# Products of weights with values of all four key tiles in one run behind the fourth exponential, and a new hand-searched order of the work

## The chip, the cores and the metric

The kernel runs on one core of a Trainium2 chip. The metric is the device time of one execution in microseconds (us). Before the change the median of three runs is 2063.27 us (2061.38 to 2065.82). A difference of about 0.2% or more can be told from no change.

The core has five engines, each of which takes its instructions in the order in which they stand in its own queue: TensorE (PE in the profile, its weight loads PEld), VectorE (DVE), ScalarE (ACT), GpSimd (POOL) and SyncE (SP, which here issues DMAs).

## The reference

Sixteen sequences of 512 positions with 256 features pass through one block, all in float32. Cut to what matters:

```python
x = x + attn(layernorm(x))      # 16 heads of 16 features, causal, softmax over the keys
x = x + ffn(layernorm(x))       # base product, shared and routed low-rank parts, 2 of 6 experts
x = x + ssm(layernorm(x))       # convolution, gates, scan over 512 positions with 16 states
x = x + ffn(layernorm(x))

# inside attn, for each head
scores = q @ k.T * scale        # masked above the diagonal
attn   = softmax(scores)
out    = attn @ v
```

The change concerns the inside of `attn`. The rest of the block matters because its operations stand in the same queues.

## The kernel before, in words

**Tiling.** A sequence is four tiles of 128 positions. The 16 heads are worked on in four groups of four heads (index `j`, `G = 4` heads). Keys and queries stand transposed in `kT` and `qT`, with the 16 features of a head in a strip of 32 partitions of its own, so four heads can use four row strips of TensorE's array at the same time.

**Scores.** The helper `four` (line 560) makes one batch of scores: four matmuls of 32 rows, one for each head (line 566, row strips), and four bfloat16 matmuls with the identity that add the causal mask (line 568, the whole array). All go to one PSUM tile named `sc`. This tile takes four of the eight PSUM banks and there is **one** of it: `banks = {"one": (4, ...), "sc": (1, ...)}`. The next batch can only start when the reader of the last one has finished. Each batch is made twice. In the first pass (mask_q, queries on the partitions, lines 628 to 640) VectorE reduces the batch to its maximum `negm` (line 637). The maxima go through a transpose (line 645) into the queries `qm` (line 650). In the second pass (mask_k, keys on the partitions, line 587 ff.) ScalarE takes the exponential of the batch and writes it to `pt0` to `pt3`, one SBUF buffer for each key tile (line 585). By causality the batches of the four key tiles have 512, 384, 256 and 128 columns a head. A sequence has 16 batches of the first kind and 16 of the second.

**Products with values.** Behind each exponential stands an operation `weigh` (line 588): four matmuls, one for each head, whose outputs go to four column strips of 32 partitions of one PSUM tile `one` (line 590, named `av`). Key tile 0 starts the sum, key tile 3 ends it. ScalarE then copies the sums to `avs` (line 596), TensorE transposes them (line 601) and VectorE divides (lines 608 and 609).

The array is thus used in three ways: in row strips (line 566), in column strips (line 590, the sums of the scan at line 874, and a small product at line 474 with 32 rows out), and whole (everything else on TensorE).

**Scan.** For each sequence, 32 groups of rows are fetched from DRAM (line 849), GpSimd multiplies (lines 856 and 867), ScalarE takes exponentials (line 861), VectorE runs the scan (line 864) and TensorE adds up (line 874).

**Order of the work.** Nothing runs in the order in which it is written. `Plan.op` records every operation with its engine, an estimated cost in microseconds (helpers `dve`, `act`, `pool`, `pe` at lines 459 to 470 and numbers beside the calls), what it reads and writes, and which buffers it takes. `Plan.order` (line 126) then walks through a model of the five engines: whenever one is free, it gives it the ready operation with the lowest turn whose buffers are free. The turn of an operation is `STARTS[sequence] + TURNS[number in the sequence]`; both tables stand in the file and were found by a search. Around a score batch an engine can be reserved: `o.then` names who is to go next, and another operation may delay that by at most `OVER` us (`kept`). `CHANGE` is a penalty in turns on an operation that needs another table of ScalarE. The instructions are issued in the order that this walk gives, and each engine keeps it.

Of the kernel before, what the change touches and what calls it, by code (L numbers as in the profile page):

```python
# [17 lines left out]
P = 128  # L18
NEG = -1.0e30


OVER, CHANGE = 2.3, 97.0
STARTS = (
    0, 149, 234, 338, 413, 521, 619, 700, 790, 888, 996, 1074, 1174, 1263, 1369, 1447,
)
TURNS = (
# [20 lines left out]
)  # L47
# [16 lines left out]
class Op:  # L64
    __slots__ = ("eng", "cost", "lat", "fn", "bufs", "after", "left", "seq", "turn", "num", "table", "load", "port", "then", "stage")


class Plan:
# [14 lines left out]

    def op(self, eng, cost, fn, r=(), w=(), lat=None, table=None, load=0.0, also=(), port=False):


        o = Op()
        o.eng, o.cost, o.fn, o.seq, o.num, o.table, o.load = eng, cost, fn, self.seq, len(self.ops), table, load
        o.lat = {"PE": 0.08, "ACT": 0.05, "SP": 2.0}.get(eng, 0.12) if lat is None else lat
        o.after, o.left, o.bufs = [], 0, []  # L90
        before = {}
        for things, writes in ((r, False), (w, True)):
            for thing in things:
                buf, part = thing if isinstance(thing, tuple) else (thing, None)
                if buf not in o.bufs:
                    o.bufs.append(buf)
                    buf.users += 1
                for p, (ws, rs) in buf.done.items():
                    if part is None or p is None or p == part:
                        for x in ws + (rs if writes else []):  # L100
                            before[x.num] = x
                ws, rs = buf.done.setdefault(part, ([], []))
                if not writes:
                    rs.append(o)
                elif part is None:
                    buf.done = {None: ([o], [])}
                else:
                    buf.done[part] = ([o], [])
        for buf in also:
            if buf not in o.bufs:  # L110
                o.bufs.append(buf)
                buf.users += 1
        before.pop(o.num, None)
        o.port, o.then, o.stage = port, None, self.stage
        for x in before.values():
            x.after.append(o)
            o.left += 1
        self.ops.append(o)
        return o
# [6 lines left out]
    def order(self):  # L126

        first = {}
        for o in self.ops:
            o.turn = STARTS[o.seq] + (TURNS or [0] * len(self.ops))[o.num - first.setdefault(o.seq, o.num)]  # L130
        free, busy, table, link, port = dict(self.places), {}, None, 0.0, False
        kept = {}
# [8 lines left out]
        while True:  # L141
            for eng, heap in ready.items():
# [28 lines left out]
                if o.table is not None:  # L171
                    cost += 1.3 * (o.table != table)
                    table = o.table
                if until is not None and self.wanted(o, what):
                    del kept[eng]
# [48 lines left out]
def tile_block(ctx: ExitStack, tc: tile.TileContext, a: dict, out: bass.AP):  # L224
# [231 lines left out]
    def rows(g):  # L456
        return slice(32 * g, 32 * g + 32)
# [4 lines left out]
    def act(n):  # L462
        return 0.2 + n / 1200.0

# [3 lines left out]
    def pe(n, k=1, extra=0.02):  # L468

        return k * 2 * (n / 1200.0 + extra)  # L470
# [28 lines left out]
    def turned(xh, xt, c, at, also=()):  # L499

        one = psum("one")

        def turn():
            for t in range(NT):
                nc.tensor.transpose(one()[:, cols(t)], xh()[:, t, cols(c)], ident)  # L505

        op("PE", 0.66, turn, r=[xh], w=[one], also=[xt, *also])
        op("ACT", act(512), lambda: nc.scalar.copy(xt()[:, c, at : at + T], one()), r=[one], w=[(xt, c)])
        return one
# [28 lines left out]
    def attention(b, x):  # L538
# [9 lines left out]
        for t in range(0, NT, 2):  # L548
# [5 lines left out]

            op("PE", pe(256, 4) + 0.2, value, r=[xt], w=[one], also=[vals])
            op("ACT", act(512), lambda t=t, one=one: nc.scalar.copy(
# [3 lines left out]
        def four(lhsT, rhs, at, mask, n, reads, into):  # L560
# [8 lines left out]

            o = op("PE", pe(n, 1, 0.09) + 0.45, run, r=reads, w=[sc], also=[into])  # L570
            return sc, o
# [3 lines left out]
        def weights_values(j, kT, qm):  # L575

            av, avs = psum("one"), sbuf("avs")
            for kt in range(NT):
                n = T - kt * P
                pt = sbuf(f"pt{kt}")  # L580
                sc, o = four(
# [5 lines left out]

                def weigh(kt=kt, pt=pt, av=av, j=j):
                    for g in range(G):
                        nc.tensor.matmul(  # L590
                            av()[rows(g), kt * P : T], lhsT=vals()[:, kt, G * j + g, :], rhs=pt()[:, g, :],
                            start=kt == 0, stop=kt == NT - 1,
                        )

                op("PE", pe(n, 1, 0.1), weigh, r=[pt, vals], w=[av], also=[avs])
            op("ACT", act(512), lambda avs=avs, av=av: nc.scalar.copy(avs(), av()), r=[av], w=[avs])
# [5 lines left out]

            op("PE", 0.66, back, r=[avs], w=[at], also=[o_tok])

# [8 lines left out]

            op("DVE", 0.72, divide, r=[at], w=[(o_tok, j)])

        for i in range(NJ // 2):
# [30 lines left out]
            qms = [sbuf("qm"), sbuf("qm")]  # L647
            op("PE", 0.66, turn, r=[nm], w=[one], also=qms)
            for s, qm in enumerate(qms):
# [7 lines left out]
        for c in range(NC):  # L657
# [5 lines left out]

            op("PE", 0.66, turn, r=[(o_tok, j) for j in range(NJ) if j * NC // NJ == c], w=[one], also=[oT])
            op("ACT", act(512), lambda c=c, one=one: nc.scalar.copy(oT()[:, c, :], one()), r=[one], w=[(oT, c)])
# [8 lines left out]
    def routed(x):  # L674
# [39 lines left out]

        op("DVE", 0.65, logits, r=[m1], w=[one])
        op("ACT", 0.25, lambda: nc.scalar.activation(ex(), lg(), AF.Exp), r=[one], w=[ex], table="exp")
# [5 lines left out]

        op("DVE", 0.65, first, r=[b1], w=[one, o1])

# [8 lines left out]

        op("DVE", 1.5, second, r=[ex, o1, m2, b2], w=[one])

# [7 lines left out]

        op("DVE", 1.3, shares, r=[ex, z, rz], w=[one, w7])
        op("DVE", 0.65, lambda: nc.vector.tensor_tensor(
# [10 lines left out]
        hT = sbuf("hT")  # L756
        op("PE", 0.66, turn, r=[hs], w=[pt], also=[hT])
        op("ACT", act(512), lambda: nc.scalar.copy(hT(), pt()[0 : NU + 1, :]), r=[pt], w=[hT])
# [7 lines left out]
    def scan(b, x):  # L766
# [71 lines left out]
        for c in range(NC):  # L838
            sums = psum("one")
            for m in range(4):  # L840
# [36 lines left out]

                op("PE", pe(512, 1, 0.18), add, r=[four[0], four[2]], w=[sums])

# [70 lines left out]
```

## Time and profile before

| | |
|---|---|
| median of 3 runs | 2063.27 us (2061.38 to 2065.82) |
| the profiled execution's own time | 2066.51 us |
| its span, first to last instruction | 2064.7 us |
| busy PE / PEld / DVE / ACT / POOL | 1801.9 / 953.8 / 1513.4 / 1194.0 / 1371.1 us |
| mean granted TensorE clock | 0.954 |
| DMA | 316.35 MB, mean 153 GB/s |

The profile gives times in us from the span's start. `L566` is line 566 of the kernel. A row such as `PE L566 MATMUL sc<-qm,kT 32*128 32x384 f32 x8` reads: matmuls of line 566 that write the tile `sc` from `qm` and `kT`, 32 rows and 128 columns of the array, a moving operand of 384 columns in float32, eight of them. A float32 matmul leaves two records, so eight records are the four matmuls of one batch. Matmuls overlap, and their ends are modelled; what one operation costs TensorE is therefore read here from the **start** of its first matmul to the start of the next operation's first. Some matmul records are missing from the trace.

### The profile page before, as it was taken

What the parts mean: (1) busy time and instruction counts of PE and PEld (TensorE: products, weight loads), DVE (VectorE), ACT (ScalarE), POOL (GpSimd) and SP (SyncE); (2) the same over time, 40 slices, a digit from 0 to 9 for tenths busy, and PEclk for the clock granted to TensorE, in tenths of its full rate; (3) what the DMA queues carried; (4) which work ended last, traced back from release to release, by engine and by line L of the source; (5) the groups of instructions that cost most, each with busy time, mean ns of one, the idle gap of its engine ahead of it and who ended that gap; (6) DMA issues with size and microseconds to landing.
All of it is one profiled execution on the core that took longest, in us unless ns stands there. A gap on an engine that the chain in (4) does not pass through costs nothing. (4 is left out here: it accounts for less than half of the span.)

```text
span 2064.7 us, 34733 instructions
## 1 busy us (share of the span) xinstructions
PE 1801.9 (87%) x13253; PEld 953.8 (46%) x13253; DVE 1513.4 (73%) x2479; ACT 1194.0 (58%) x1685; POOL 1371.1 (66%) x814
## 2 busy tenths in 40 slices
PE   4788789999999999999999999999999999996455
PEld 2244344555455454545455454545554454544123
DVE  4335677878788787878788787878788787876563
ACT  2236556565666757565666667575666766564431
POOL 3001784949587685859597785859596785848693
PEclk8789899999999999999999999999999999998766
DMA  3000956848494866847494867849493957747791
GB/s 93 1 1 22 216 122 155 197 127 210 109 233 109 216 164 167 205 137 191 110 231 100 225 153 175 204 120 212 110 231 95 228 143 186 183 125 183 186 222 31
DMA packets 113064, 316.35 MB, mean 153 GB/s; under 512 B 17809, under 2 KB 36610, under 8 KB 112898
## 3 DMA queue, kind: packets, MB, share of 16 engines
q1 hardware_dynamic: 112194, 313.99, 62.5%
q8 instruction: 105, 1.72, 0.4%
q14 instruction: 61, 0.50, 0.1%
q10 hardware_dynamic: 704, 0.14, 0.0%
HBM read 287.87 MB, written 26.21 MB: 152 GB/s over the span
## 5 line engine op out<-in xcount | busy, mean ns | idle before, releaser
L864 DVE TENSOR_TENSOR_SCAN dd<-one,dd 128x512 f32<-128x512 f32 x512 | 607.9, 1212 | 185.2 <-ACT one L861 88.3
L856 POOL TENSOR_TENSOR dd<-dd,bc 128x1024 f32<-128x1024 f32 x256 | 603.6, 2361 | 194.0 <-DMA dd<-drows 156.8
L867 POOL TENSOR_TENSOR dd<-dd,bc 128x1024 f32<-128x1024 f32 x256 | 601.9, 2358 | 86.2 <-DVE dd L864 80.4
L637 DVE TENSOR_REDUCE negm<-sc 128x4 f32<-128x512 f32 (+3 forms) x256 | 380.4, 1486 | 154.0 <-PE sc L568 153.7
L861 ACT ACTIVATE one<-dd,am 128x512 f32<-128x512 f32 x512 | 344.3, 689 | 249.4 <-DVE dd L864 108.9
L585 ACT ACTIVATE pt<-sc 128x2048 f32<-128x2048 f32 (+3 forms) x256 | 316.3, 1235 | 189.0 <-PE sc L568 187.8
L487 POOL TENSOR_SCALAR rs<-mv 128x4 f32<-128x4 f32 x64 | 12.3, 193 | 364.2 <-DVE mv L482 361.4
L566 PE MATMUL sc<-qm,kT 32*128 32x512 f32 (+3 forms) x2048 | 214.1, 488 | 37.8 <-ACT pt L585 28.4
L566 PE MATMUL sc<-kT,qT 32*128 32x128 f32 (+3 forms) x2048 | 217.0, 494 | 30.5 <-DVE negm L637 25.9
L568 PEld LDWEIGHTS <-identb 128*128 128x128 bf16 x2048 | 117.4, 98 | 232.4 <-issue 217.2
L874 PE MATMUL one<-dd,ysel 128*32 128x512 f32 x1024 | 172.7, 633 | 55.5 <-POOL dd L867 46.4
L590 PE MATMUL one<-pt,vv 128*32 128x512 f32 (+3 forms) x2048 | 191.6, 449 | 8.1 <-DVE dd L864 7.9
L566 PEld LDWEIGHTS sc<-qm,kT 32*128 32x128 f32 x2048 | 80.9, 185 | 181.5 <-ACT pt L585 120.4
L474 PE MATMUL one<-base,xtR 128*128 128x256 f32 x512 | 139.5, 395 | 18.6 <-DVE dd L864 18.0
L566 PEld LDWEIGHTS sc<-kT,qT 32*128 32x128 f32 x2048 | 82.0, 187 | 156.8 <-DVE negm L637 63.3
L494 ACT ACTIVATE xhR<-x,nm,rs 128x256 f32<-128x256 f32 x192 | 99.4, 588 | 53.2 <-POOL nm L490 53.1
L528 DVE TENSOR_TENSOR x<-one,x 128x512 f32<-128x512 f32 x128 | 86.4, 675 | 34.7 <-PE one L474 34.5
L474 PEld LDWEIGHTS one<-base,xtR 128*128 128x128 f32 x512 | 94.5, 194 | 36.8 <-DVE dd L864 21.5
L481 DVE BATCH_NORM_STATS2 st<-x 128x6 f32<-128x256 f32 x256 | 103.7, 405 | 4.8 <-DMA x<-in_x_dram 4.1
L568 PE MATMUL sc<-mask_q,identb 128*128 128x128 bf16 x1024 | 103.7, 225 | 0.0
L568 PE MATMUL sc<-mask_k,identb 128*128 128x128 bf16 x1024 | 102.8, 224 | 0.0
L505 PE MATMUL one<-ident,xhR 128*128 128x128 f32 x384 | 61.9, 290 | 35.2 <-ACT xhR L494 27.7
(132 smaller groups left out, 2449.4 us busy)
## 6 DMA issues: line engine op xcount, KB each, us to landing
dd<-drows SPq DMA_DIRECT2D x512, 512.0 KB
x<-in_x_dram SPq DMA_DIRECT2D x16, 512.0 KB
drows<-dt SPq DMA_DIRECT2D x32, 256.0 KB
drows<-sg SPq DMA_DIRECT2D x32, 256.0 KB
bc<-brows SPq DMA_DIRECT2D x16, 512.0 KB
out_dram<-x SPq DMA_DIRECT2D x16, 512.0 KB
brows<-few SPq DMA_DIRECT2D x16, 64.0 KB
wo<-in_Wo_dram SPq DMA_DIRECT2D x2, 256.0 KB
```

The costliest lines, as they stand in the source:

```text
L474: nc.tensor.matmul(o[:, lo:hi], lhsT=lhsT, rhs=rhs, start=n == 0, stop=n == len(todo) - 1)
L481: nc.vector.bn_stats(st()[:, t, :], x()[:, t, :])
L566: nc.tensor.matmul(sc()[:, g, 0:n], lhsT=lhsT(g), rhs=rhs(g), start=True, stop=False)
L568: nc.tensor.matmul(sc()[:, g, at : at + P], lhsT=identb, rhs=mask, start=False, stop=True)
L585: o.then = op("ACT", act(G * n), lambda pt=pt, sc=sc, n=n: nc.scalar.activation(pt(), sc()[:, :, 0:n], AF.Exp), r=[sc], w=[pt], table="exp")
L590: nc.tensor.matmul(av()[rows(g), kt * P : T], lhsT=vals()[:, kt, G * j + g, :], rhs=pt()[:, g, :], start=kt == 0, stop=kt == NT - 1,)
L637: o.then = op("DVE", dve(G * n), lambda t=t, n=n, sc=sc, nm=nm, s=s: nc.vector.tensor_reduce(nm()[:, t, :, 1 - s, 0:1], sc()[:, :, 0:n], A ...
L856: op("POOL", pool(1024), lambda dd=dd: nc.gpsimd.tensor_tensor(dd()[:, :, 1, :], dd()[:, :, 1, :], both(0), ALU.mult), port=True, r=[(bc, ...
L861: op("ACT", act(512) + 0.07, lambda i=i, k=k, dd=dd, dec=dec: nc.scalar.activation(dec(), dd()[:, i, 0, :], AF.Exp, scale=am[:, k + 4 * i ...
L864: op("DVE", 1.22, lambda i=i, dd=dd, dec=dec: nc.vector.tensor_tensor_scan(dd()[:, i, 1, :], dec(), dd()[:, i, 1, :], 0.0, ALU.mult, ALU.a ...
L867: op("POOL", pool(1024), lambda dd=dd: nc.gpsimd.tensor_tensor(dd()[:, :, 1, :], dd()[:, :, 1, :], both(1), ALU.mult), port=True, r=[(bc, ...
L874: nc.tensor.matmul(sums()[rows(g), :], lhsT=ysel[:, m, :], rhs=four[g]()[:, g % 2, 1, :], start=m == 0, stop=m == 3)
```

## The change

Each exponential had its product `weigh` behind it. Now the four products of a group of heads are one operation of 16 matmuls that reads all four of `pt0` to `pt3`. The matmuls, their shapes and their number are the same. The planner's costs are new numbers for many operations, its model of TensorE takes 0.2 us off an operation of "columns" mode behind another one, `OVER` goes from 2.3 to 1.7, `CHANGE` from 97 to 60, and both tables of turns are new. The core of the diff:

```diff
-OVER, CHANGE = 2.3, 97.0
+OVER, CHANGE = 1.7, 60.0
 STARTS = (
...
+                if eng == "PE":
+                    cost -= 0.2 * (o.mode is not None and o.mode == mode)
+                    mode = o.mode
...
     def act(n):
-        return 0.2 + n / 1200.0
+        return 0.17 + n / 1200.0
...
-        op("PE", 0.66, turn, r=[xh], w=[one], also=[xt, *also])
+        op("PE", 0.57, turn, r=[xh], w=[one], also=[xt, *also])
...
-            o = op("PE", pe(n, 1, 0.09) + 0.45, run, r=reads, w=[sc], also=[into])
+            o = op("PE", pe(n, 1, 0.0) + 0.5, run, r=reads, w=[sc], also=[into])
...
             av, avs = psum("one"), sbuf("avs")
+            pts = [sbuf(f"pt{kt}") for kt in range(NT)]
             for kt in range(NT):
                 n = T - kt * P
-                pt = sbuf(f"pt{kt}")
+                pt = pts[kt]
...
-                def weigh(kt=kt, pt=pt, av=av, j=j):
+            def weigh():
+                for kt in range(NT):
                     for g in range(G):
                         nc.tensor.matmul(
-                            av()[rows(g), kt * P : T], lhsT=vals()[:, kt, G * j + g, :], rhs=pt()[:, g, :],
+                            av()[rows(g), kt * P : T], lhsT=vals()[:, kt, G * j + g, :], rhs=pts[kt]()[:, g, :],
                             start=kt == 0, stop=kt == NT - 1,
                         )

-                op("PE", pe(n, 1, 0.1), weigh, r=[pt, vals], w=[av], also=[avs])
+            op("PE", 2.2 + 0.2, weigh, r=pts + [vals], w=[av], also=[avs], mode="columns")
...
-                op("PE", pe(512, 1, 0.18), add, r=[four[0], four[2]], w=[sums])
+                op("PE", pe(512, 1, 0.18), add, r=[four[0], four[2]], w=[sums], mode="columns")
```

The remaining edits are costs of the planner alone (a few hundredths to 0.2 us each, as in the third and fourth hunk), and the tables `STARTS` and `TURNS`. They change no instruction, only the order.

More of the change, by code (lines that the diff above doesn't have):

```diff
@@ L19 @@
 NEG = -1.0e30
-OVER, CHANGE = 2.3, 97.0
+OVER, CHANGE = 1.7, 60.0
 STARTS = (
-    0, 149, 234, 338, 413, 521, 619, 700, 790, 888, 996, 1074, 1174, 1263, 1369, 1447,
+    0, 363, 754, 1360, 1140, 1792, 2114, 2484, 3089, 2828, 3285, 3687, 3986, 4332, 4709, 4877,
 )
 TURNS = (
[20 rows of a table removed]
[22 rows of a table added]
 )
@@ L64 @@
 class Op:
-    __slots__ = ("eng", "cost", "lat", "fn", "bufs", "after", "left", "seq", "turn", "num", "table", "load", "port", "then", "stage")
+    __slots__ = ("eng", "cost", "lat", "fn", "bufs", "after", "left", "seq", "turn", "num", "table", "load", "port", "then", "stage", "mode")
 class Plan:
@@ L82, in buf, with op @@
         return Buf(self, res, make)
-    def op(self, eng, cost, fn, r=(), w=(), lat=None, table=None, load=0.0, also=(), port=False):
+    def op(self, eng, cost, fn, r=(), w=(), lat=None, table=None, load=0.0, also=(), port=False, mode=None):
         o = Op()
@@ L113, in op @@
         before.pop(o.num, None)
-        o.port, o.then, o.stage = port, None, self.stage
+        o.port, o.then, o.stage, o.mode = port, None, self.stage, mode
         for x in before.values():
@@ L130, in order @@
             o.turn = STARTS[o.seq] + (TURNS or [0] * len(self.ops))[o.num - first.setdefault(o.seq, o.num)]
-        free, busy, table, link, port = dict(self.places), {}, None, 0.0, False
+        free, busy, table, link, port, mode = dict(self.places), {}, None, 0.0, False, None
         kept = {}
@@ L553, in value @@
                     products(one()[:, i * D : (i + 1) * D], [(xt()[:, c, cols(t + i)], wv[:, c, :], 0, D) for c in range(NC)])
-            op("PE", pe(256, 4) + 0.2, value, r=[xt], w=[one], also=[vals])
+            op("PE", pe(256, 4), value, r=[xt], w=[one], also=[vals])
             op("ACT", act(512), lambda t=t, one=one: nc.scalar.copy(
@@ L601, in back @@
                     nc.tensor.transpose(at()[:, cols(t)], avs()[:, cols(t)], ident)
-            op("PE", 0.66, back, r=[avs], w=[at], also=[o_tok])
+            op("PE", 0.57, back, r=[avs], w=[at], also=[o_tok])
             def divide(at=at, j=j):
@@ L612, in divide @@
                 )
-            op("DVE", 0.72, divide, r=[at], w=[(o_tok, j)])
+            op("DVE", 0.68, divide, r=[at], w=[(o_tok, j)])
         for i in range(NJ // 2):
@@ L647, in attention @@
             qms = [sbuf("qm"), sbuf("qm")]
-            op("PE", 0.66, turn, r=[nm], w=[one], also=qms)
+            op("PE", 0.57, turn, r=[nm], w=[one], also=qms)
             for s, qm in enumerate(qms):
@@ L662, in turn @@
                     nc.tensor.transpose(one()[:, cols(t)], o_tok()[:, t, cols(c)], ident)
-            op("PE", 0.66, turn, r=[(o_tok, j) for j in range(NJ) if j * NC // NJ == c], w=[one], also=[oT])
+            op("PE", 0.57, turn, r=[(o_tok, j) for j in range(NJ) if j * NC // NJ == c], w=[one], also=[oT])
             op("ACT", act(512), lambda c=c, one=one: nc.scalar.copy(oT()[:, c, :], one()), r=[one], w=[(oT, c)])
@@ L713, in logits @@
             nc.vector.tensor_tensor(lg(), lg(), wide(m1()), ALU.subtract)
-        op("DVE", 0.65, logits, r=[m1], w=[one])
+        op("DVE", 0.57, logits, r=[m1], w=[one])
         op("ACT", 0.25, lambda: nc.scalar.activation(ex(), lg(), AF.Exp), r=[one], w=[ex], table="exp")
@@ L721, in first @@
             nc.vector.tensor_tensor(o1(), k1(), wide(b1()), ALU.is_equal)
-        op("DVE", 0.65, first, r=[b1], w=[one, o1])
+        op("DVE", 0.55, first, r=[b1], w=[one, o1])
         def second():
@@ L732, in second @@
             nc.vector.tensor_tensor(lg(), lg(), o1(), ALU.add)
-        op("DVE", 1.5, second, r=[ex, o1, m2, b2], w=[one])
+        op("DVE", 1.33, second, r=[ex, o1, m2, b2], w=[one])
         def shares():
@@ L742, in shares @@
             nc.vector.tensor_tensor(w7()[:, :, 0:E], lg(), wide(rz()), ALU.mult)
-        op("DVE", 1.3, shares, r=[ex, z, rz], w=[one, w7])
+        op("DVE", 1.1, shares, r=[ex, z, rz], w=[one, w7])
         op("DVE", 0.65, lambda: nc.vector.tensor_tensor(
@@ L756, in routed @@
         hT = sbuf("hT")
-        op("PE", 0.66, turn, r=[hs], w=[pt], also=[hT])
+        op("PE", 0.57, turn, r=[hs], w=[pt], also=[hT])
         op("ACT", act(512), lambda: nc.scalar.copy(hT(), pt()[0 : NU + 1, :]), r=[pt], w=[hT])
```

42 rows, old and new, of the table TURNS are left out of this document.

## Prediction

> **What bounds the kernel now.** I read the page's slices first, then the busy time by stretch, then the waits of TensorE in the even middle, then TensorE's order of time.
>
> ```profile
> PE   4788789999999999999999999999999999996455
> ...
> PEclk8789899999999999999999999999999999998766
> ```
>
> ```profile
> 600.00:1755.00 1155.00, 1087.82 (x8284) 581.11 (x8280) 936.18 (x1521) 740.95 (x1051) 853.70 (x500) 1.00 0.70 170
> 0.00:300.00 300.00, 225.63 (x1634) 113.41 (x1635) 148.07 (x261) 126.65 (x169) 95.02 (x77) 0.87 0.31 75
> 1843.00:2065.00 222.00, 123.76 (x576) 66.20 (x576) 121.78 (x207) 83.49 (x123) 157.04 (x81) 0.74 0.68 162
> ```
>
> The columns are PE, PEld, DVE, ACT, POOL, then clock and DMA. TensorE bounds the middle: 1087.8 of 1155 us busy at full clock, DVE 936, POOL 854, ACT 741. Ten sequences pass there: the first of a sequence's exponentials of scores comes every 115.5 us (mean of ten). Head and tail are looser. The chain of waits, taken from the end, covers the tail alone, so I work with TensorE's queue. Its longest wait in the middle is
>
> ```profile
> PE sc L566 <- ACT pt L585: 14.2, 50, 0.4
> ```
>
> that is, a score batch waiting for the exponential of the batch before it. Here is what stands around such waits:
>
> ```profile
> 1731.96 0.93 PE L566 MATMUL sc<-qm,kT 32*128 32x384 f32 x8 [0.20 <-ACT pt L585]
> 1732.82 0.40 PE L568 MATMUL sc<-mask_k,identb 128*128 128x128 bf16 x4
> 1733.80 1.06 PE L590 MATMUL one<-pt,vv 128*32 128x512 f32 x8 [0.58 <-DVE dd L864]
> 1734.80 0.71 PE L566 MATMUL sc<-qm,kT 32*128 32x256 f32 x8
> 1735.45 0.40 PE L568 MATMUL sc<-mask_k,identb 128*128 128x128 bf16 x4
> 1735.77 0.85 PE L590 MATMUL one<-pt,vv 128*32 128x384 f32 x8
> 1736.96 0.50 PE L566 MATMUL sc<-qm,kT 32*128 32x128 f32 x8 [0.33 <-ACT pt L585]
> ```
>
> From the 256-column batch (1734.80) to the next (1736.96) are 2.16 us. TensorE's own batch takes 0.97 of them; a product with values fills most of the rest. That product is **filler** while the one `sc` tile is being read.
>
> **What the change saves: switches.** Costs are taken start to start:
>
> ```profile
> 1000.68 0.40 PE L568 MATMUL sc<-mask_k,identb 128*128 128x128 bf16 x4
> 1001.01 0.85 PE L590 MATMUL one<-pt,vv 128*32 128x384 f32 x8
> 1001.68 1.04 PE L874 MATMUL one<-dd,ysel 128*32 128x512 f32 x8
> ...
> 1005.21 0.40 PE L568 MATMUL sc<-mask_q,identb 128*128 128x128 bf16 x4
> 1005.45 1.29 PE L505 MATMUL one<-ident,xhR 128*128 128x128 f32 x8
> ```
>
> A mask run takes 0.33 before column strips and 0.24 before the whole array; medians over the trace are 327 and 234 ns, so entering a strip mode costs 93 ns. The 384-column product takes 669 ns before other column-strip work (0.67 above) and 783 before whole-array work, 114 ns for leaving. The 256-column one has 456 and 570, the same 114. A run of column strips thus costs 207 ns beyond its work.
>
> The built order of both kernels (counted, no time in it) has the same 8,227 matmuls. Runs of column strips fall from 346 to 189; entries into row strips straight from whole-array work rise from 310 to 382. Sum: 157 x 0.207 = 32.5 saved, 72 x 0.093 = 6.7 given back, **25.8 us less TensorE work**. In the even middle, a sequence has 22 runs before and 12 after, 19 entries and 23: 2.07 - 0.37 = 1.70 us less. A run of four products (512, 384, 256, 128 columns) should take 0.88 (996 ns alone, less 114) + 0.67 + 0.46 + 0.36 = 2.37 us; four lone ones take 1.00 + 0.78 + 0.57 + 0.36 = 2.71. The joint behind 512 columns is too rare in the trace to show; between no gain and the 114 ns I take the latter, by the two joints it does show.
>
> [...]
>
> ScalarE loads its tables 16 times less (68 to 52, 1.283 us each, 20.5 us). ScalarE is idle a third of the middle, so I count it as nothing; if a load stood ahead of an exponential that a score batch waits for, it would be at most those 20.5. The products issue no DMA. All queues are reordered, SP's and GpSimd's among them, but the counts are equal, and before the first scan (133 against 138 us of TensorE work) and behind the last score batch (136 against 138 us of GpSimd work) they stand alike.
>
> **What it costs: the filler is gone.** A score batch can't start before the reader of the last one has finished. The shortest start-to-start times with that bound, from the trace, are for exponentials (512, 384, 256, 128 columns) 3.44, 2.80, 2.16, 1.52 us, and for maxima 3.86, 3.11, 2.36, 1.62. The batch itself, with both switches, is 1.40, 1.19, 0.97, 0.76 of each. The rest must be filled by whatever the order has between, or TensorE stands. I went through both orders, added the durations of everything between two batches, and took the shortfall.
>
> Even middle, one sequence, before: two batches of 512 (0.29, 0.32), one of 384 (0.61), two of 256 (0.40 each), two of 128 (0.19 each): 2.39 us. After: twice a batch of 384 and then one of 256 follow with **nothing** between: 2 x (2.80 - 1.19 + 2.16 - 0.97) = 5.58; a 512-maximum with only transposes (0.71); 0.32, 0.31, 0.20 and 0.17 elsewhere: 7.29 us. So a sequence costs 4.90 more in waits and 1.70 less in switches: **+3.19 us**.
>
> As a check, the same sum for before is 111.25 of work + 2.39 = 113.64 us; the trace has 115.5. The 1.9 us left are waits for other data, such as line 474 for VectorE. After: 116.83, or 118.7 with the same 1.9.
>
> The whole, to the last-but-one scan's start: before 1684.8 + 70.8 = 1755.6, after 1655.6 + 152.7 = 1808.3 us. Of the difference of **52.7**, 15.8 come from the head (up to the third scan 42.1 against 64.8 us of shortfall, 6.9 less work), 35.2 from eleven even sequences, 1.7 from the one after. Behind that point 160 us of GpSimd work stand in both orders, and I count zero.
>
> The profiled execution took 2066.5 (span 2064.7 and 1.8 around it), 3.2 above the median. 2066.5 + 52.7 - 3.2 = **2116 us**.
>
> The new wait for all four exponentials stands at the products. Behind it is all of TensorE's queue, the next score batch first. In 46 of 64 runs a later score batch stands between the fourth exponential and the products. In the other 18, about one a sequence, it is mostly a 512-column batch whose exponential ends 3.4 us from the batch's start, and 3.55 us of work stand there (1.31 + 1.72 + 0.44 + 0.09). So I price it at nothing; bounds are no gain and, if such an exponential starts its own length late, 18 x 1.87 = 34 us. The wait for other data (1.9 a sequence) is not shown for the new order: it can vanish under the longer score waits (-22 over twelve sequences) or double (+22).
>
> [...]
>
> **Rivals.**
> 1. *The waits swallow each other.* Waits for `sc` give other data time, the 1.9 vanish, and the head loses only half its 15.8: 2116 - 22 - 8 = 2086. For it: those waits name VectorE, idle 219 of 1155 us, which could catch up while TensorE stands. Against: VectorE has waits of its own for score batches, which come later too.
> 2. *The end pays* (other side: faster). In 1843 to 2065 GpSimd is busy 157 of 222 us, so 65 could go; the last slices show TensorE at 4 to 6 tenths. It decides from 53 us on; if all 65 went, 2116 - 65 = 2051. Against: the order there has the same GpSimd work, and GpSimd's waits there are for fetched rows first (22.6 us), which the change leaves alone.
> 3. *Score turnarounds don't bind, switches do*: 2063.3 - 25.8 = 2037. It needs a 384-column exponential to hand back `sc` in under 1.2 us, where it lasts 1.45 itself. That the change doesn't cut switches is excluded by the count.
> 4. *New waits*, on VectorE or behind the fourth exponential: 2116 + 22 to 34, near 2145.
>
> **Numbers.** Forecast 0.67 (2100 to 2132), rival 1 0.13, rival 4 0.08, near no change 0.03, rival 2 0.06, rival 3 0.03. A measurement here tells about 0.2% from no change. Faster 0.09, same 0.03, slower 0.88. The range 2083 to 2145 takes in rivals 1 and 4 and leaves out about 0.14.
>
> **What would show it.** Right: about 190 runs of column strips, 0.88/0.67/0.46 inside a run; score batches of 384 and 256 columns 2.8 and 2.2 us before the next with TensorE idle; its waits for `pt` well above 14 us in a like stretch; a period near 118.7 us; the tail unchanged. Wrong: a period under 115.5, or a tail (last-but-one scan to end, 221 us) shorter by tens.

## The result, and the profile after

After the change: 2153.23 us (2152.66 to 2156.31, four runs) against 2064.55 for before (2061.38 to 2065.90, four runs), a ratio of 1.0435 (1.0417 to 1.0453). The forecast was 2116 with a range up to 2145: slower, as said, but by 88.7 us instead of 52.7, and outside the range. From one scan to the next a sequence takes 120.7 us (mean of eleven; 115.4 before); the forecast was 118.7.

First the two rows of the page's slices for after.

```profile
PE   5688888898989899998889899898988899987634
...
PEclk8689998999999999999999999999999999997766
```

Before had a 9 in every slice of the middle's PE row; now 8s stand among them. The clock's digits look alike, since they stop at 9. The busy time by stretch (same columns as before: PE, PEld, DVE, ACT, POOL, clock, DMA) shows what they hide.

```profile
600.00:1755.00 1155.00, 1046.98 (x7927) 591.42 (x7926) 890.08 (x1448) 697.00 (x995) 830.84 (x479) 0.95 0.69 165
0.00:300.00 300.00, 219.63 (x1552) 114.03 (x1553) 136.43 (x233) 117.49 (x157) 84.07 (x72) 0.84 0.29 70
1927.00:2151.00 224.00, 131.18 (x600) 72.34 (x596) 120.51 (x210) 81.18 (x122) 157.12 (x81) 0.71 0.66 158
```

In the even middle the granted clock is 0.95 where it was 1.00, and TensorE is busy 1047 us of 1155 where it was 1088. Its longest wait, in the same stretch:

```profile
PE sc L572 <- ACT pt L592: 62.8, 50, 1.7
```

This is the wait of a score batch for the exponential before it, 14.2 us before; none is longer than 1.7 us. A score batch that is followed by the next one with nothing between is called bare here. TensorE's order of time at one such place in after:

```profile
604.69 0.93 PE L572 MATMUL sc<-qm,kT 32*128 32x384 f32 x8
605.55 0.40 PE L574 MATMUL sc<-mask_k,identb 128*128 128x128 bf16 x4
607.62 0.71 PE L572 MATMUL sc<-qm,kT 32*128 32x256 f32 x8 [1.67 <-ACT pt L592]
608.27 0.40 PE L574 MATMUL sc<-mask_k,identb 128*128 128x128 bf16 x4
609.78 0.81 PE L572 MATMUL sc<-qm,kT 32*128 32x128 f32 x8 [1.11 <-ACT pt L592]
610.52 0.60 PE L574 MATMUL sc<-mask_k,identb 128*128 128x128 bf16 x4
610.92 3.07 PE L480 MATMUL one<-low,xtR 128*128 128x118 f32 x16
613.92 0.50 PE L572 MATMUL sc<-kT,qT 32*128 32x128 f32 x8
614.36 0.40 PE L574 MATMUL sc<-mask_q,identb 128*128 128x128 bf16 x4
614.68 2.36 PE L599 MATMUL one<-pt,vv 128*32 128x512 f32 x32
```

The pair of bare batches is there as forecast: 384 columns to the next batch 2.93 us here, 256 to the next 2.16. Behind it the same instructions take longer: four mask matmuls 0.60 instead of 0.40, and the product of `low` 3.00 us to the next start, where it takes 1.93 before a score batch at full clock. The trace grants half clock from 609.7 to 613.2. At 614.68 the clock is back, and the run of four products takes 2.29 us to the next start, which is also the median at full clock.

**Where the 86 us between the two spans went.** I laid the built order beside the trace and gave each operation its duration at full clock, switches included. What half clock adds while it lasts is "clock"; the rest of the time is a wait, sorted by whether a score batch comes next. In us:

| stretch | kernel | work | clock | score waits | other waits |
|---|---|---|---|---|---|
| eleven even sequences (scan 3 to 14) | before | 1137.2 | 0 | 49.1 | 83.0 |
| | after | 1119.4 | 60.9 | 101.0 | 48.0 |
| up to the third scan | after less before | -4.4 | +20.7 | +14.5 | -8.2 |
| behind the fourteenth | after less before | -3.6 | +14.1 | +3.6 | -10.3 |

Over the whole: work -26, score waits +70, clock +96, other waits -54. The first is what was forecast; the clock isn't in the forecast at all. The clock's part doesn't hang on these durations: in after one mask matmul follows another after 56 ns at full clock and 107 at half, so about half of TensorE's busy time in the stretches of half clock is its price, by this estimate 57.1 us before and 146.0 after, 89 more. How the rest divides does hang on them: counted as plain gaps in TensorE's records, those ahead of score batches grow by 91 us and all others shrink by 28.

### The profile page after: what moved, and what is told of

Its sections match the earlier page's. It is cut to its first block, busy times and chain, and to the rows that moved or that the text cites. A ratio compares the mean times of both kernels' runs of the same rounds, so it can differ in the third digit from the quotient of the medians.

```text
span 2150.7 us, 34758 instructions
## 1 busy us (share of the span) xinstructions
PE 1824.9 (85%) x13253; PEld 1012.9 (47%) x13253; DVE 1504.8 (70%) x2479; ACT 1178.5 (55%) x1669; POOL 1374.8 (64%) x814
## 5 line engine op out<-in xcount | busy, mean ns | idle before, releaser
L873 DVE TENSOR_TENSOR_SCAN dd<-one,dd 128x512 f32<-128x512 f32 x512 | 603.4, 1211 | 168.5 <-ACT one L870 105.6
L876 POOL TENSOR_TENSOR dd<-dd,bc 128x1024 f32<-128x1024 f32 x256 | 602.6, 2359 | 77.6 <-DVE dd L873 62.1
L646 DVE TENSOR_REDUCE negm<-sc 128x4 f32<-128x1536 f32 (+3 forms) x256 | 378.9, 1480 | 134.2 <-PE sc L574 133.0
L592 ACT ACTIVATE pt<-sc 128x512 f32<-128x512 f32 (+3 forms) x256 | 317.1, 1239 | 194.7 <-PE sc L574 194.1
L572 PE MATMUL sc<-qm,kT 32*128 32x384 f32 (+3 forms) x2048 | 233.4, 529 | 120.3 <-ACT pt L592 95.3
L493 POOL TENSOR_SCALAR rs<-mv 128x4 f32<-128x4 f32 x64 | 12.5, 195 | 470.0 <-DVE mv L488 466.9
L572 PE MATMUL sc<-kT,qT 32*128 32x128 f32 (+3 forms) x2048 | 219.5, 500 | 38.6 <-DVE negm L646 20.7
L574 PEld LDWEIGHTS <-identb 128*128 128x128 bf16 x2048 | 122.9, 101 | 245.6 <-issue 234.1
L572 PEld LDWEIGHTS sc<-qm,kT 32*128 32x128 f32 x2048 | 87.8, 201 | 248.8 <-ACT pt L592 140.7
L883 PE MATMUL one<-dd,ysel 128*32 128x512 f32 x1024 | 160.8, 668 | 37.7 <-POOL dd L876 37.7
L599 PE MATMUL one<-pt,vv 128*32 128x512 f32 (+3 forms) x2048 | 157.9, 450 | 1.5 <-ACT pt L592 1.5
L500 ACT ACTIVATE xhR<-x,nm,rs 128x256 f32<-128x256 f32 x192 | 102.2, 592 | 57.2 <-POOL nm L496 57.1
L574 PE MATMUL sc<-mask_k,identb 128*128 128x128 bf16 x1024 | 110.9, 237 | 0.0
L511 PE MATMUL one<-ident,xhR 128*128 128x128 f32 x384 | 66.0, 305 | 49.1 <-DVE dd L873 25.6
```

The source lines that it names most:

```text
L572: nc.tensor.matmul(sc()[:, g, 0:n], lhsT=lhsT(g), rhs=rhs(g), start=True, stop=False)
L574: nc.tensor.matmul(sc()[:, g, at : at + P], lhsT=identb, rhs=mask, start=False, stop=True)
L592: o.then = op("ACT", act(G * n), lambda pt=pt, sc=sc, n=n: nc.scalar.activation(pt(), sc()[:, :, 0:n], AF.Exp), r=[sc], w=[pt], table="exp")
L599: nc.tensor.matmul(av()[rows(g), kt * P : T], lhsT=vals()[:, kt, G * j + g, :], rhs=pts[kt]()[:, g, :], start=kt == 0, stop=kt == NT - 1,)
L646: o.then = op("DVE", dve(G * n), lambda t=t, n=n, sc=sc, nm=nm, s=s: nc.vector.tensor_reduce(nm()[:, t, :, 1 - s, 0:1], sc()[:, :, 0:n], A ...
L873: op("DVE", 1.22, lambda i=i, dd=dd, dec=dec: nc.vector.tensor_tensor_scan(dd()[:, i, 1, :], dec(), dd()[:, i, 1, :], 0.0, ALU.mult, ALU.a ...
```

## The experiments

The expectations weigh three theories. W: only the waits of score batches cost. C: these waits also bring the low clock, and the low clock costs too. T: the new tables of turns are what costs, not the merge.

### The merge apart from the order

**merge_old**: the merge with the old tables.

```diff
-                op("PE", pe(n, 1, 0.1), weigh, r=[pt, vals], w=[av], also=[avs])
+            op("PE", 2.4, weigh, r=pts + [vals], w=[av], also=[avs])
```

> The kernel before with the merge alone: one run of four products behind the fourth exponential, with the turns of the fourth product; the tables of turns, costs, OVER and CHANGE are those of before. In its order runs of column strips fall from 346 to 190, and the sum of work and score shortfalls rises from 1853.9 to 1910.7 us. Theory W (waits for the score tile alone): about +57 us, near 2121. Theory C (these waits also halve the TensorE clock for stretches of 3.4 to 6.8 us behind them): about +57 and 25 to 35 more, near 2150, with 20 to 45 such stretches between 480 and 1800 us where the kernel before has none. Theory T (the new tables are what costs, the merge gains its switches): near 2040.

Measured: 2318.66, ratio 1.1239 (1.1209 to 1.1268). No theory had this. The walk, given turns that were made for a program with 12 more operations a sequence, gives an uneven order (up to 154 us from scan to scan, and 110 loads of ScalarE's tables instead of 68). The run thus says nothing of the merge, only that tables of turns don't carry over to another program.

**held**: before's own order of everything, in which a product is kept back until the group's last one.

```diff
+                    group["wait"].append((kt, pt))
+                    if group["hold"] and len(group["wait"]) < NT:
+                        return
...
+                    for k, p in todo:
                         for g in range(G):
```

> The merge alone in the exact order of before: the planner runs as before, but the products of a group are kept back and issued together where its fourth product stood (a group is left as it is where the next group's exponential into the same buffer stands before that place). Every other instruction keeps its place on its engine. Runs of column strips 346 to 194. By the corrected sum (transposes counted once) work falls by 20.2 us and score shortfalls rise by 86.9 (3.7 to 9.5 us a sequence). Theory 'filler' (the merge takes the filler out of the score gaps, whatever the tables): 50 to 95 us slower than before, near 2065 + 67 = 2132 and up to 2160 with low-clock stretches. Theory T (the new tables cost, the merge itself pays its switches): 2040 to 2050.

Measured: 2182.32, ratio 1.0571 (1.0547 to 1.0594). The merge alone costs 119 us, more than the 50 to 95 expected; the new tables and planner costs give about 29 of it back. So the tables aren't what costs. In the even middle: work 1123.1, clock 72.5, score waits 119.8, other 43.3. TensorE's order of time in held:

```profile
606.88 0.71 PE L567 MATMUL sc<-qm,kT 32*128 32x256 f32 x8 [1.54 <-ACT pt L587]
607.53 0.40 PE L569 MATMUL sc<-mask_k,identb 128*128 128x128 bf16 x4
609.08 0.50 PE L567 MATMUL sc<-qm,kT 32*128 32x128 f32 x8 [1.15 <-ACT pt L587]
609.51 0.61 PE L569 MATMUL sc<-mask_k,identb 128*128 128x128 bf16 x4
610.81 2.09 PE L567 MATMUL sc<-qm,kT 32*128 32x512 f32 x8 [0.69 <-ACT pt L587]
612.83 0.60 PE L569 MATMUL sc<-mask_k,identb 128*128 128x128 bf16 x4
613.37 3.81 PE L598 MATMUL one<-pt,vv 128*32 128x512 f32 x32
```

Three waits in a row, then a 512-column batch in 2.56 us instead of 1.4 and a run of four products in 3.63 instead of 2.29: half clock again (granted from 609.5 to 616.3).

### Is it the waits for the exponential?

**short_exp**: after, with shorter exponentials of key tiles 1 and 2 (the edit is shown shortened).

```diff
-nc.scalar.activation(pt(), sc()[:, :, 0:n], AF.Exp)
+nc.scalar.activation(pt()[:, 0:h, :], sc()[:, 0:h, 0:n], AF.Exp)     # h = 1 for kt in (1, 2), else 4
```

> The changed kernel, same order, with the exponentials of key tiles 1 and 2 (384 and 256 columns) done for one head of four; the other heads' weights stay at a constant, so three quarters of these exponentials are left out. The turnaround of a 384-column batch falls from 2.80 to about 1.83 us, of a 256-column one from 2.16 to 1.52; the sum of work and shortfalls falls from 1911.1 to 1853.2. Theory W: 58 us less than the changed kernel, near 2095. Theory C: the low-clock stretches go as well, near 2065 to 2070. If ScalarE's load counts too, lower still.

Measured: 2108.82, ratio 1.0222 (1.0192 to 1.0251), 44 us less than after. Score waits fell from 101.0 to 62.1 and clock from 60.9 to 33.7 in the even middle, 66 us together, but other waits rose from 48.0 to 88.6. The wait list (us in total, times, longest) in 600 to 1755:

```profile
PE sc L576 <- ACT pt L596: 24.1, 48, 0.7
PE one L515 <- DVE dd L877: 19.4, 20, 1.2
PE one L767 <- DVE hsc L758: 16.5, 20, 1.2
```

TensorE waits for VectorE's `hsc` 16.5 us, 4.4 in after. Both theories missed this: the time that a score wait takes is in part time in which other data become ready.

**double_exp**: before, with the exponentials of key tiles 1 and 2 done twice (shortened).

```diff
-nc.scalar.activation(pt(), sc()[:, :, 0:n], AF.Exp)
+[nc.scalar.activation(pt(), sc()[:, :, 0:n], AF.Exp) for _ in range(2 if kt in (1, 2) else 1)]
```

> The kernel before, same order and products unmerged, with the exponentials of key tiles 1 and 2 done twice over into the same buffer (no other value). The turnaround of a 384-column batch becomes about 4.25 us, of a 256-column one 3.18; score shortfalls rise from 2.39 to 8.37 us a sequence, in all +99 us. Theory W: near 2163, clock 1.0 in the middle. Theory C: waits of 1.2 to 2.1 us follow each other here as well, so low-clock stretches appear in the middle without any merged run, and the time is 20 to 50 us more: near 2200. If the low clock came from runs of column strips or from the new order, none appear.

Measured: 2182.57, ratio 1.0573 (1.0540 to 1.0605). Nine stretches of half clock, 37.5 us, stand in the even middle, where before has none: neither the merge nor the new order is needed for them, only longer waits of score batches. The price lies between the two theories; in the even middle score waits grew by 72, the clock cost 20, and other waits fell by 19.

### Does the low clock cost time, and what keeps it up?

**warm**: after, with idle matmuls (nobody reads them) in the bare gaps, wherever any bank is free.

```diff
+            if o in bare and o.spare > 0:
+                idle = ps.tile([P, 512], F32, tag="one", name="idle", bufs=banks["one"][0])
+                for _ in range(o.warm):          # 22 behind 384 columns, 14 behind 256
+                    nc.tensor.matmul(idle[:, 0:P], lhsT=identb, rhs=mask_k, start=True, stop=True)
```

> The changed kernel, same order, with idle matmuls (bfloat16, 128 columns, into a free PSUM bank that nobody reads) in 41 of the 67 gaps in which a score batch of keys is followed by another with nothing between: 22 behind a batch of 384 columns, 14 behind one of 256. They are shorter than the wait and change nothing that is computed. Theory W: no gain, 2153 or up to 5 more. Theory C: where idle matmuls stand, the low-clock stretch behind is gone, elsewhere it stays; about half of the 126 us of low clock in the even middle goes, and 10 to 18 us of time: near 2139.

Measured: 2159.03, ratio 1.0461 (1.0433 to 1.0489): no gain, though half clock fell from 126 to 96 us; the 2139 of theory C didn't come. In 15 of the 41 gaps the idle matmuls took the last bank that was free by the plan. First TensorE's, then ScalarE's order of time in warm:

```profile
604.66 1.39 PE L924 MATMUL idle<-mask_k,identb 128*128 128x128 bf16 x22
608.85 0.71 PE L574 MATMUL sc<-qm,kT 32*128 32x256 f32 x8 [2.79 <-ACT pt L595]
```

```profile
606.74 0.69 ACT L873 ACTIVATE one<-dd,am 128x512 f32<-128x512 f32 x1 [1.82 <-DVE dd L876]
607.36 1.43 ACT L595 ACTIVATE pt<-sc 128x1536 f32<-128x1536 f32 x1
```

The scan's exponential (L873), which writes to a bank, stands ahead of the score exponential (L595) and comes late: its wait ends with the scan (L876), which reads another such bank out. So the score batch waits 2.79 us. This is once a sequence 5.28 us from batch to batch instead of 2.80, 27 us over eleven. With that, the experiment didn't separate the theories.

**warm2**: the same only where two banks are free (26 gaps instead of 41).

```diff
-            if o in bare and o.spare > 0:
+            if o in bare and o.spare > 1:
```

> As the run with idle matmuls, but only in gaps where two or more PSUM banks were free by the plan (26 of 67; in the even middle the 14 behind one of the two 256-column batches). The run before had put 22 idle matmuls into the last free bank, and the exponential behind stood 2.5 us longer once a sequence; this takes that away. Theory C: low-clock stretches behind that gap shrink, 3 to 12 us below the changed kernel, 2141 to 2150. Theory W: 2153.

Measured: 2124.44, ratio 1.0293 (1.0273 to 1.0314): **29 us less than after by instructions that compute nothing**. In the even middle half clock fell from 126 to 78.5 us, its cost from 60.9 to 39.3. The low clock costs time. Theory C had only 3 to 12 us. Of the 26 us between the two spans 11 come from the even middle and 12 from the stretch ahead of the third scan, where half clock fell from 120 to 75 us.

**warm_loads**: after, with idle weight loads in all 67 bare gaps.

```diff
+            if o in bare:
+                for _ in range(o.warm):          # 24 behind 384 columns, 16 behind 256
+                    nc.tensor.ldweights(identb)
```

> The changed kernel, same order, with idle weight loads (identity, bfloat16, 57 ns each in the trace) in all 67 bare score gaps: 24 behind a 384-column batch, 16 behind a 256-column one, shorter than the wait; no PSUM bank is taken, nothing computed changes. Theory C (the low clock follows idle of TensorE and costs time): if weight loads count as activity, the low-clock stretches between 480 and 1800 us mostly go, and 15 to 35 us: 2120 to 2138. If weight loads don't count for the clock, the stretches stay and the time is 2153. Theory W (the low clock is hidden by the waits): stretches go, time stays within 5 us of 2153.

Measured: 2154.59, ratio 1.0444 (1.0424 to 1.0463), as after. Weight loads in the gap, then the product of `low` (3.46 us to the next start, 1.93 at full clock), in warm_loads:

```profile
485.77 1.02 PEld L921 LDWEIGHTS <-identb 128*128 128x128 bf16 x24
```

```profile
491.39 3.53 PE L482 MATMUL one<-low,xtR 128*128 128x118 f32 x16
```

Half clock in the even middle is 136.5 us (126 in after), where warm2 with idle matmuls in 26 of the gaps has 78.5: here the weight loads didn't keep the clock, and the matmuls did in part.

**fill**: after, with real products in the gap: where a bare gap has two banks free, those of the group whose weights are there.

```diff
+            if o in bare and o.spare > 1:
+                o.fill()        # weigh() up to the first key tile whose exponential isn't issued yet
```

> The changed kernel, but where a 256- or 384-column score batch is followed by nothing but the next score batch, the products of the same group whose weights are already there are put behind it, if two banks are free; the group's remaining products stay together behind its last exponential. In the even middle that is one gap of four in each sequence, the third-tile one, with the products of tiles 0 and 1 (1.7 us by the rows, where the gap is 1.2 us): runs of column strips rise from 189 to 208, the sum of shortfalls falls by 1.14 us a sequence and the switches cost 0.11 more. Theory W (the missing filler costs its shortfall and nothing more): 12 x 1.0 plus 7 of the head, 2153 - 15 to 20 = 2133 to 2138, low clock as before. Theory C (the idle gap also brings the low clock; closing one of a sequence's two pairs of gaps leaves one stretch of low clock where there were two): a further 20 to 25 us, near 2112, and less than 80 us of low clock in the middle where the changed kernel has 126. Idle matmuls in the same gap gave 2124; real products in their place should be faster than that under C, and slower under W.

Measured: 2136.20, ratio 1.0365 (1.0344 to 1.0386): 17 us less than after. The time is W's, though the place isn't: score waits hardly moved in the even middle (102.6), where the clock's cost fell by 12. Of the 12.5 us between the two spans 6 come from the head and 6 from the even middle. Half clock stayed at 22 stretches, 99 us, between 600 and 1800 (after: 23, 113 us). In fill:

```profile
599.83 0.71 PE L577 MATMUL sc<-qm,kT 32*128 32x256 f32 x8 [1.67 <-ACT pt L605]
600.48 0.40 PE L579 MATMUL sc<-mask_k,identb 128*128 128x128 bf16 x4
600.80 2.94 PE L614 MATMUL one<-pt,vv 128*32 128x512 f32 x16
```

The filled gap is gone, but its two products (1.64 us to the next start at full clock) take 2.88: half clock from 601.1 on, after one wait of 1.67 us. That a pair of waits is the trigger, as theory C had it, fell with this.

**What triggers it.** In each of the 13 traces the edges of the low stretches lie on a grid of 3.413 us (in before and after to within 4 ns, the stretches being 1 to 12 such windows long). I took TensorE's busy share (matmul records) in every window of that grid, and the clock of the window after it, all traces together:

| window at full clock, busy | next at half | | window at half clock, busy | next at half |
|---|---|---|---|---|
| under 0.45 | 311 of 312 | | under 0.75 | 467 of 467 |
| 0.45 to 0.50 | 51 of 69 | | 0.75 to 0.85 | 103 of 110 |
| 0.50 to 0.55 | 85 of 163 | | 0.85 to 0.95 | 28 of 85 |
| 0.55 to 0.60 | 16 of 137 | | 0.95 and over | 2 of 392 |
| 0.60 and over | 3 of 6283 | | | |

So in these traces a full-clock window under 0.50 busy was followed by one at half clock in 362 of 381 cases, one of 0.60 and over in 3 of 6283; behind a half-clock window of 0.95 and over full clock was back in 390 of 392 cases, behind one under 0.85 in 7 of 577. In after, 606.3 to 609.7 is 0.31 busy, and 609.7 to 613.2 runs at half clock; in fill, 597.7 to 601.1 is 0.51. From 600 to 1700 the least busy window of before has 0.59, and none falls; after has 22 of 322 under 0.55.

### Two tests with the rule

**held_free**: held, but only for the 50 of 256 products whose gap stays filled without them.

```diff
+                    if w.hold:          # 50 products, listed
+                        return
+                    todo, group["wait"] = group["wait"], []
```

> The kernel before, same order, with 50 of its 256 products kept back to the next product of their group, only where the score gap they leave stays longer than the turnaround of the batch before it. Runs of column strips 346 to 318, work 4.6 us less, score shortfalls the same. Theory 'filler': 3 to 6 us faster than before (0.15 to 0.3%), no low clock in the middle. If merging costs by itself (a run of products later for its copy, buffers held longer): no gain or slower.

Measured: 2057.68, ratio 0.9973 (0.9959 to 0.9987), 5.7 us less than before, with 318 runs of column strips for 346. The forecast's price of a switch gives the same (28 x 0.207 = 5.8; the interval allows 2.7 to 8.5), so a part of the merge pays. Its least busy window is 0.61, and the middle has no half clock.

**free_warm** and **free_warm9**: held_free with idle matmuls in head and tail, 0.6 or 0.9 of each gap that the planner sees.

```diff
+            if o.eng == "PE" and o.gap > 0.6 and o.spare > 1:
+                idle = ps.tile([P, 512], F32, tag="one", name="idle", bufs=banks["one"][0])
+                for _ in range(int(0.6 * o.gap / 0.057)):
+                    nc.tensor.matmul(idle[:, 0:P], lhsT=identb, rhs=mask_k, start=True, stop=True)
```

> held_free (the kernel before with 50 products kept back where a filler can be spared, 2057.68 us, ratio 0.9973) with idle bf16 matmuls (their result is never read) put into TensorE's gaps of head and tail where the planner sees a gap above 0.6 us and at least two banks free; 0.6 of the gap is filled. The middle has no such place. In held_free's trace the clock is at half for 58 us up to the third scan and for 119 us behind the fourteenth. The traces so far put the low clock on a grid of windows of 3.413 us: a window in which TensorE is busy for less than about half is followed by one at half clock, and full clock comes back after a window that is over about 0.85 busy. Theory C (that is the rule): the low stretches of head and tail shrink by a third or more, and the head, where TensorE sets the pace, gains 5 to 12 us: 2045 to 2053. Theory W (idle matmuls are only in the way, or the head waits for loads and maxima): 2056 to 2065.

> The same with 0.9 of each such gap filled. Theory C: fewer low stretches still, 2042 to 2052, unless the idle matmuls run over their gap, which at half clock they do (113 ns for 56): then back towards 2058. Theory W: 2060 to 2070.

Measured: 2039.70, ratio 0.9892 (0.9874 to 0.9910), and 2042.51, ratio 0.9899 (0.9883 to 0.9916). Both beat both kernels: the first by more than theory C had, the second at the fast end of its range. The stretches of free_warm and then of held_free:

```profile
0.00:200.00 200.00, 162.41 (x1544) 97.10 (x1548) 86.47 (x178) 79.73 (x104) 23.48 (x43) 1.00 0.15 40
200.00:450.00 250.00, 227.84 (x1763) 119.26 (x1755) 191.64 (x297) 155.53 (x218) 178.57 (x100) 0.98 0.69 164
```

```profile
0.00:200.00 200.00, 144.90 (x1066) 73.81 (x1067) 79.77 (x172) 77.09 (x101) 23.38 (x42) 0.91 0.11 28
200.00:450.00 250.00, 221.44 (x1671) 115.40 (x1669) 189.34 (x282) 147.52 (x208) 169.54 (x96) 0.96 0.68 161
```

Half clock up to the third scan falls from 58 to 10 us, and GpSimd's first multiplication of that scan begins at 436.9 instead of 450.1, 13 of the 16 us between the two spans. Behind the fourteenth it falls from 119 to 68 us, for 2 us: TensorE isn't the bound there. The fuller variant has less half clock still (46 us there) and isn't faster. The 113 ns expected of an idle matmul at half clock is twice its 56; mask matmuls of the same form in after have 107.

## Why the prediction was right and wrong

**Right: the switches.** 25.8 us less work were forecast; the accounting has 26. The joint behind 512 columns does pay its 114 ns: from start to start a run of four products has 0.88, 0.65 and 0.43 us (forecast 0.88, 0.67 and 0.46) and costs 2.29 us in all, forecast 2.37.

**Right: the turnarounds.** A bare batch of 384 columns is followed after 2.80 us (12 times) or 2.93 (10 times), one of 256 after 2.16 (19 of 22 times); forecast 2.80 and 2.16. Score waits rose by 52 us over eleven sequences, forecast 4.90 x 11 = 54; as plain gaps they rose by 64. The filler is gone, as said, though the nearness of these two sums is in part luck (below).

**Right: the tail.** In 1927 to 2151 GpSimd is busy 157.1 us, as before's 157.0 in its tail; from the last-but-one scan on, 221.0 became 223.3 us.

**Failed: the step "a sequence costs 4.90 more in waits and 1.70 less in switches: +3.19".** It priced every operation at full clock and took an idle gap at its own length. The row that it rested on, a clock of 1.00 in the even middle, is one of before's order and not of the chip: before's least busy window is 0.59. In after each sequence has two stretches of half clock, 26 in eleven sequences, 60.9 us, and head and tail lose 35 more; the head's 15.8 us were priced in the same way, and it is 23 us longer. That this costs time is shown by warm2 (-29 us by idle matmuls), and that low windows bring it by the table and by free_warm (58 to 10 us of half clock up to the third scan, once idle matmuls stand in the gaps). The forecast could have had it. In before's own trace every full-clock window under 0.50 busy, all of them in head and tail, is followed by half clock (14 of 14), and none of the 524 over 0.55 is. And bare waits of 1.61 and 1.19 us around a batch of 0.97 make 2.8 us idle of 3.8, less than half busy.

**Failed: "the 1.9 us left are waits for other data".** A transpose leaves one record on TensorE (1152 in before's trace for the 72 in each of 16 sequences), not two as a float32 product does (eight for the four of a score batch), and the forecast priced it as two: 72 a sequence at 0.11 us are 7.9 us of work that isn't there. Mended, before has 103.4 of work and about 8 of other waits a sequence, not 1.9. They were priced as unchanged; they fell by 35 us in the even middle and by 54 in all. Rival 1 (the waits swallow each other) was thus real and larger than its price of 30, and it hid a part of the clock's cost; short_exp shows the same from the other side. The mended sums make a sequence about 4.2 us longer instead of 3.19 and the whole about 71 (97 of shortfall, 26 less work). Of those 97 only 70 appear as score waits, other waits give back 54, the clock adds 96: 71 - 27 - 54 + 96 = 86. So the number 52.7 was off by less than its parts: a cost that was left out and a saving that was left out partly cancel, and that is luck.

**The other rivals.** Rival 2 (the end pays) didn't happen: the tail is 2 us longer. Rival 3 is refuted by the turnarounds and the time. Rival 4 named 2145, near the time, but for a wait behind the fourth exponential: waits of products for `pt` are 1.5 us in the whole run, so the new wait is free, as priced; and TensorE's waits for VectorE in 600 to 1755 are 40 us in all, 37 before.

**Open.** In these traces the change to half clock sets in between 0.45 and 0.60 busy (311 of 312 windows below, 3 of 6283 above), not sharper, since matmul ends are modelled. (No record is missing in before or after: the 8,227 matmuls give 13,253 records, two for a float32 product, one for a mask or a transpose.) Busy time may not be the right measure either. Of the full-clock windows between 0.45 and 0.55, 72 of the 87 that are row-strip matmuls for 0.3 or more of their time are followed by half clock, and 8 of the 49 with less than 0.1. Whether a matmul on a part of the array counts for less was not tested. Why real products in a gap (fill, 99 us of half clock) kept the clock less well than idle whole-array matmuls in the same gap (warm2, 68 us between 600 and 1800) wasn't tried further.

## What to carry to other kernels

Before a stall is added to a kernel that holds full clock, lay windows of 3.413 us, the grid of these traces, over TensorE's order and look for those that fall under about half busy. Here 22 of 322 fell under 0.55 between 600 and 1700 us, none before; over the whole run score waits cost 70 us more and half clock 96, while other waits shrank by 54. Work that seems to sit in the way of a batch may be what keeps the clock; take away only what leaves its gap filled (held_free, 50 of 256 products kept back: 5.7 us less and no half clock in the middle), and where a gap can't be filled with work, idle matmuls into a spare bank can pay (free_warm, 1.1% under before). Where a sum of work and waits closes with little left, check the size of its largest term on single records first.

## What the runs showed of the hardware that was not expected

In the 13 traces half clock followed windows of 3.413 us in which TensorE was under 0.50 busy (362 of 381), and was over behind windows of 0.95 busy and more (390 of 392). In after two waits around one batch (1.67 and 1.11 us) stood ahead of 3.4 us at half clock; from 600 to 1755 us 13 of its 23 low stretches have 3.4 us and 10 have 6.8. In fill one wait of 1.67 us stood ahead of such a stretch.

With idle bfloat16 matmuls in 26 gaps (140 of them, 11.8 us, between 600 and 1800 us) half clock in the even middle fell from 126 us in after to 78.5 in warm2; with weight loads (24 in 1.02 us) in all 67 bare gaps it was 136.5 in warm_loads.
